# Two-by-two block products with seven multiplications for the outputs of the last three token blocks

## The chip, the cores and the metric

The kernel runs on one core of a Trainium2 chip. The core has five engines with queues of their own: TensorE (PE, matmuls, with its weight loads shown separately as PEld), VectorE (DVE), ScalarE (ACT), GpSimd (POOL) and SyncE (SP, which issues the DMAs). The metric is the time of one execution on the device in microseconds; lower is better. PE reads its operands from the on-chip buffer SBUF and writes sums to PSUM, which has banks of 512 float32 values per partition; POOL works on SBUF only.

## The reference

The program is one transformer layer on 2 x 1024 tokens of width 512: attention, then a gated feed-forward network with weights that are quantised and expanded again, each followed by a normalisation and a residual. Only its last step bears on the change:

```python
    def _L0_ffn_ref(x, w1, w2, w3):
        ...
        gate = jnp.einsum('bsd,hd->bsh', x, dq1)
        up = jnp.einsum('bsd,hd->bsh', x, dq2)
        h = jax.nn.silu(gate) * up
        return jnp.einsum('bsh,dh->bsd', h, dq3)
    x = L0_attn_hidden_states
    x = x + _layernorm(_L0_attn_ref(_layernorm(x, axis=-1), L0_attn_Wq, L0_attn_Wk, L0_attn_Wv, L0_attn_Wo), axis=-1)
    x = x + _layernorm(_L0_ffn_ref(_layernorm(x, axis=-1), L0_ffn_w1, L0_ffn_w2, L0_ffn_w3), axis=-1)
```

The hidden width is 1376, that is ten blocks of 128 and an eleventh of 96. All of it is float32.

## The kernel before

Attention comes first and takes about 1670 us; the feed-forward part after it is the class FeedForward, whose method run drives everything from there on. It goes over four token blocks of 512 tokens (tb = 0 to 3, called block 0 to block 3). Each block has a hidden part and an output part.

In the hidden part, for each of the eleven blocks f of hidden features, the method hidden computes gate and up for 512 tokens. It is already a product of two-by-two blocks by seven multiplications (Strassen's scheme in Winograd's form): seven products, each of two matmuls with 256 columns, on sums of weights (weight_sums, four POOL instructions per f) and sums of tokens (token_sums, four POOL instructions of 512 columns per token block, into the tiles T and into one quarter of the block's transposed tokens xnT). The results, times the sigmoid, become hT[f], 128 hidden features by 512 tokens. The last operation of each f, which multiplies the high half of hT[f] on POOL, is issued one step late, after the next products have begun; for f = 10 it is issued at the end of the hidden part, and token_sums for the next block follows it in POOL's queue.

In the output part, the method outputs takes 128 tokens at a time: eleven matmuls of 512 columns, `lhsT=self.hT[f][:n, m * P : (m + 1) * P]`, `rhs=self.w3[f][:n, :]`, into a bank of the pool "out", then puts three steps into the list later: the statistics of the row (DVE, with a power of -1/2 on POOL, rstd), the normalisation into the row buffer res (DVE), and the addition of the residual yacc with the DMA to the result (DVE, SP). run takes these steps out of later between PE's products; at the end of an output part up to three are left for the first hidden row of the next block, at i = 0, 2 and 4.

PE, DVE, ACT and POOL each work in the order of the program here: every call goes through a wrapper (InOrder) that keeps it. So an instruction waits for its own operands and for everything before it on its engine. The instructions all carry line 117, the wrapper's; operations are told apart by the names of tiles. Names that occur: wos, wkv, wq, ffq, ffqtmp, ffqr, ffqs, ffs are reused buffers that now hold T and hT; wdown, ffqh and ffa hold w3; ffoc is res; pgate, pup, pout and ptr are the PSUM pools "gate", "up", "out" and "tr", of two banks each.

Of the kernel before, what the change touches and what calls it, by code (L numbers as in the profile page):

```python
# [13 lines left out]
F32R = mybir.dt.float32r  # L14
I32 = mybir.dt.int32
AF = mybir.ActivationFunctionType
ALU = mybir.AluOpType
# [4 lines left out]
P = 128  # L22
# [6 lines left out]
KT = HID // P  # L29
CB = 2  # L30
FF = 1376
# [89 lines left out]
def sandwich_kernel(ctx: ExitStack, tc: tile.TileContext, x, wq, wk, wv, wo, w1, w2, w3, out, con):  # L121
    nc = tc.nc
    x = x.rearrange("b n d -> (b n) d")
    out = out.rearrange("b n d -> (b n) d")
# [14 lines left out]
    yacc = keep.tile([P, NCI, HID], F32)  # L139

    xnT = keep.tile([P, KT, T], F32)
# [11 lines left out]
    def norm_stats(src, vector=nc.vector, gpsimd=nc.gpsimd):  # L153

        st = small.tile([P, 6], F32)
        vector.bn_stats(st, src)
        mv = small.tile([P, 2], F32)
        vector.bn_aggr(mv, st)
        ve = small.tile([P, 1], F32)
        vector.tensor_scalar(ve, mv[:, 1:2], EPS, None, ALU.add)  # L160
        rstd = small.tile([P, 1], F32)
        gpsimd.tensor_tensor(rstd, ve, mhalf, ALU.pow)
        return mv[:, 0:1], rstd

    def normed(dst, src, vector=nc.vector, stats=None):
        mean, rstd = stats or norm_stats(src, vector)
        vector.tensor_scalar(dst, src, mean, rstd, ALU.subtract, ALU.mult)
# [131 lines left out]
    def fast_attention():  # L299

        with ExitStack() as attn:
# [6 lines left out]
            q2p = attn.enter_context(tc.tile_pool(name="fq2p", bufs=2))  # L308
# [8 lines left out]
            product = tensor.matmul  # L317
# [5 lines left out]
            def parts_tile(name):  # L323
                return wop.tile([P, 2, GRP, HID], F32R, tag="wop", name=name)
# [85 lines left out]
            keys, Q, S = {}, {}, {}  # L410
# [300 lines left out]
            F = FeedForward((pmm, "mm"), (psc, "sc"), (ptr, "tr"), (po, "o"))  # L711
            early = {}

            def quarters(t):
                return t.rearrange("p i h d -> p (i h) d").bitcast(F32)

            def freed(pool, tag, count, dtype=F32, n=512):

                shape = {F32R: [P, GRP, P], BF16: [P, 576]}.get(dtype, [P, n])
                tiles = [pool.tile(shape, dtype, tag=tag, name=f"ff{tag}{i}", bufs=count) for i in range(count)]  # L720
                if dtype == F32R:
                    return [t.rearrange("p h t -> p (h t)").bitcast(F32) for t in tiles]
                return tiles
# [48 lines left out]
            for n in range(N_):  # L772
                g, b, c = chunks[n]
# [3 lines left out]
                more, keys2 = n + 1 < N_, n + CB < N_  # L777
# [112 lines left out]
            more = [columns(four[:, j, :]) for j in range(4)]  # L890
# [12 lines left out]
            down = quarters(parts_tile("wdown"))  # L903
            for f, t in enumerate([down[:, j, :] for j in range(8)] + freed(q2p, "qh", 2) + freed(q2p, "a", 1)):
                F.w3[f] = t
            F.res = freed(q2p, "oc", 1, F32R)
            F.run(2, 4)

    def general_attention():
# [301 lines left out]
    class FeedForward:  # L1211
# [21 lines left out]
        def next(self, name):  # L1233

            pieces = getattr(self, name)
            i = self.used.get(name, 0)
            self.used[name] = i + 1
            return pieces[i % len(pieces)]
# [152 lines left out]
        def outputs(self, ci):  # L1391
# [10 lines left out]

            self.later += [lambda: stats.append(norm_stats(pf, self.vector, self.gpsimd)), lambda: normed(res, pf, self.vector, stats[0]), added]

        def run(self, f0, ready):


            ups, downs = iter(range(ready, NFT)), iter(range(NFT))

            def loaded_up(f):  # L1410
                return None if f is None else (f, [self.load_up(i, f) for i in range(2)])

            def loaded_down(f):
                return None if f is None else (f, self.load_down(f))

            def next_down(col):
                if col:
                    self.down_weights(*col)
                return loaded_down(next(downs, None))

            row, col = loaded_up(next(ups, None)), loaded_down(next(downs, None))
            last = None
            for tb in range(T // self.TB):
                more = tb + 1 < T // self.TB

                begin = max(f0, 1) if tb == 0 else 1
                xc = self.load_tokens((tb + 1) * self.MB) if more else None
                for f in range(f0 if tb == 0 else 0, NFT):
                    if f not in self.sums:
                        list(self.weight_sums(f))  # L1430
                    products = self.hidden(tb, f)
                    sums = self.weight_sums((f + 1) % NFT) if f + 1 < NFT or more else iter(())
                    m = f - begin if more and f - begin < 2 * self.MB else -1
                    ci = (tb + 1) * self.MB + m // 2
                    if m >= 0 and m % 2 == 0:
                        self.later += self.token_parts(ci, xc)
                    for i in range(7):
                        next(products)
                        if i == 0 and last:
                            next(last)  # L1440
                        if i in (0, 2, 4) and self.later:
                            xn = self.later.pop(0)()
                        if 1 <= i <= 4:
                            next(sums, None)
                        if i == 2 and row:
                            self.up_weights(0, row[0], row[1][0])
                        if i == 4 and row:
                            self.up_weights(1, row[0], row[1][1])
                            row = loaded_up(next(ups, None))
                        if tb == 0 and (i == 5 or i == 1 and f >= NFT - f0):  # L1450
                            col = next_down(col)
                    last = products
                    if m >= 0 and m % 2 == 0:
                        xc = self.load_tokens(ci + 1) if m < 2 * (self.MB - 1) else None
                    elif m >= 0:
                        self.token_transposes(ci, xn)
                next(last)
                last = None
                if more:
                    self.token_sums(tb + 1, self.gpsimd)  # L1460
                for m in range(self.MB):
                    self.outputs(tb * self.MB + m)
                    while len(self.later) > (3 if m + 1 == self.MB and more else 0):
                        self.later.pop(0)()

    def plain_feed_forward():
        with ExitStack() as ffn:
            fp = ffn.enter_context(tc.tile_pool(name="fp", bufs=1))
            psums = [(ffn.enter_context(tc.tile_pool(name=name, bufs=2, space=PSUM)), name) for name in ("pgate", "pup", "ptw", "pout")]
            F = FeedForward(*psums)  # L1470
            quarters = [w[:, j, :] for w in wqs for j in range(4)] + [wos[:, j, :] for j in range(4)]
            quarters += list(tables.rearrange("p i (c e) d -> p (i c) (e d)", e=4)[:, j, :] for j in range(4))
            quarters += [wkv.rearrange("p (j e) d -> p j (e d)", j=2)[:, j, :] for wkv in wkvs for j in range(2)]
            for f in range(NFT):
                for w, name in ((F.w1, "w1"), (F.w2, "w2")):
                    w[f] = [fp.tile([P, KT, P], F32, name=f"{name}_{f}")]
                F.w3[f] = fp.tile([P, 512], F32, name=f"w3_{f}")
                F.hT[f] = quarters.pop() if f < 7 else fp.tile([P, 512], F32, name=f"hT_{f}")
            F.S = [[fp.tile([P, 2, P], F32, name=f"sum{i}{j}") for j in range(4)] for i in range(2)]
            F.tmp = [fp.tile([P, F.HB], F32, name=f"part{j}") for j in range(6)]  # L1480
            F.T = [quarters.pop() for _ in range(3)]
            F.xc, F.yn, F.xn, F.res = ([quarters.pop()] for _ in range(4))
            F.rows, F.cols = ([quarters.pop() for _ in range(2)] for _ in range(2))
            F.sg = [t[:, i * F.HB : (i + 1) * F.HB] for t in (quarters.pop(), quarters.pop()) for i in range(2)]
            for ci in range(F.MB):
                F.tokens(ci, F.load_tokens(ci))
                F.token_transposes(ci, F.token_norms(ci))
            F.token_sums(0, F.gpsimd)
            for f in range(2):
                for i in range(2):  # L1490
                    F.up_weights(i, f, F.load_up(i, f))
            F.scale_products()
            F.run(0, 2)
# [34 lines left out]
    with tc.If(flag != 0) as cmp:  # L1528
        fast_attention()
# [28 lines left out]
```

## Time and profile before

| | us |
|---|---|
| median of the runs (3) | 2101.16 (2100.3 to 2102.02) |
| profiled execution, its own time | 2101.61 |
| its span, first to last instruction | 2099.7 |
| PE busy in the span | 2066.5 (98%) |
| one output part (four outputs) | 37.7 |
| hidden part of blocks 1, 2, 3 | 69.3, 69.4, 66.4 |
| from the last matmul to the end | 8.3 |

The profile is of one execution. A row of the timeline gives start and duration in us, engine, source line, operation, the tile written and the tiles read, shapes (partitions x elements), and in brackets how long the engine had stood idle and what ended that. A row of the table by stretches gives the stretch, its length, and for each engine the busy time with the number of instructions. A float32 matmul appears as two records, each with its own weight load. Matmuls overlap in the pipeline, so what one costs is read from the distance between the starts of neighbours, not from its duration: records of 512 columns start 0.43 us apart and take 0.59 us each.

### The profile page before, as it was taken

What the parts mean: (1) busy time and instruction counts of PE and PEld (TensorE: products, weight loads), DVE (VectorE), ACT (ScalarE), POOL (GpSimd) and SP (SyncE); (2) the same over time, 40 slices, a digit from 0 to 9 for tenths busy, and PEclk for the clock granted to TensorE, in tenths of its full rate; (3) what the DMA queues carried; (4) which work ended last, traced back from release to release, by engine and by line L of the source; (5) the groups of instructions that cost most, each with busy time, mean ns of one, the idle gap of its engine ahead of it and who ended that gap; (6) DMA issues with size and microseconds to landing.
All of it is one profiled execution on the core that took longest, in us unless ns stands there. A gap on an engine that the chain in (4) does not pass through costs nothing.

```text
span 2099.7 us, 29474 instructions
## 1 busy us (share of the span) xinstructions
PE 2066.5 (98%) x9476; PEld 1503.1 (72%) x9476; DVE 1589.6 (76%) x3123; ACT 1394.4 (66%) x4045; POOL 1124.3 (54%) x1524
## 2 busy tenths in 40 slices
PE   7999999999999999999999999999999999999998
PEld 4777777777777777777777777777767785858584
DVE  4888888888888888888888888788887663838352
ACT  4788888887888888888888888888876340202020
POOL 5555655555566546554655574556554452626250
PEclk9999999999999999999999999999999999999999
DMA  6100100010011001000100010000011030000000
GB/s 227 36 11 26 51 16 11 21 51 10 11 40 36 12 15 41 31 11 11 58 13 11 26 58 12 11 17 22 21 36 31 26 101 21 21 20 16 21 1 22
DMA packets 48307, 64.65 MB, mean 31 GB/s; under 512 B 6736, under 2 KB 22736, under 8 KB 48144
## 3 DMA queue, kind: packets, MB, share of 16 engines
q1 hardware_dynamic: 48144, 62.68, 9.3%
q8 instruction: 77, 1.26, 0.2%
q14 instruction: 86, 0.70, 0.1%
HBM read 50.01 MB, written 12.65 MB: 30 GB/s over the span
## 4 chain that ended last, share of the span: by engine, by line
PE 86%; ACT 5%; DVE 5%; POOL 3%; issue 1%; DMA 0%; ACTq 0%; POOLq 0%; DVEq 0%
PE pq L117 18%; PE pout L117 12%; PE py L117 9%; PE pk L117 9%; PE ot L117 9%; PE pa L117 6%; PE ps L117 5%; PE pup L117 3%; PE pgate L117 3%; PE tr L117 3%; PE tq L117 2%; PE pg L117 2%; POOL qr L117 2%; ACT ps L117 1%; PE pS L117 1%
## 5 line engine op out<-in xcount | busy, mean ns | idle before, releaser
L117 POOL TENSOR_TENSOR qtmp<-q,tables 128x512 f32<-128x512 f32 x128 | 162.3, 1268 | 570.6 <-ACT q L117 570.6
L117 PE MATMUL pq<-wq,xnT 128*128 128x512 f32 x1024 | 460.7, 592 | 1.6 <-ACT xnT L117 1.6
L117 PEld LDWEIGHTS pq<-wq,xnT 128*128 128x128 f32 x1024 | 184.8, 190 | 185.4 <-issue 185.4
L117 ACT ACTIVATE zs<-xw,fbounds 128x512 bf16<-128x512 f32 (+3 forms) x416 | 287.8, 723 | 0.0
L117 PE MATMUL py<-wop,oc 128*128 128x512 f32 x1024 | 270.9, 406 | 0.0
L117 ACT ACTIVATE ps<-ps,nms 128x128 f32<-128x128 f32 x512 | 175.1, 342 | 115.4 <-DVE nms L117 101.0
L117 ACT ACTIVATE pq<-pq,nmq 128x128 f32<-128x128 f32 x512 | 175.1, 342 | 91.6 <-DVE nmq L117 79.1
L117 PE MATMUL pk<-wkv,xnT 128*128 128x256 f32 x1024 | 231.5, 379 | 0.0
L117 PEld LDWEIGHTS pk<-wkv,xnT 128*128 128x128 f32 x1024 | 194.5, 190 | 46.5 <-issue 16.3
L117 PEld LDWEIGHTS py<-wop,oc 128*128 128x128 f32 x1024 | 182.9, 189 | 35.0
L117 POOL TENSOR_TENSOR qr<-q,tables 128x256 f32<-128x256 f32 x256 | 206.3, 827 | 0.0
L117 DVE SCALAR_TENSOR_TENSOR zp<-zp,zs 128x512 f32<-128x512 f32 (+3 forms) x224 | 195.2, 871 | 9.9 <-ACT zs L117 4.7
L117 POOL TENSOR_TENSOR qr<-qr,qtmp 128x512 f32<-128x512 f32 x128 | 166.2, 1299 | 10.0
L117 DVE SCALAR_TENSOR_TENSOR zm<-zm,zs 128x512 f32<-128x512 f32 (+3 forms) x192 | 161.5, 841 | 5.0 <-ACT zs L117 2.6
L117 DVE TENSOR_TENSOR ps<-ps,fwin 128x512 f32<-128x512 f32 x128 | 89.2, 697 | 91.2 <-PE ps L117 90.8
L117 PE MATMUL ps<-kT,qrT 128*128 128x128 f32 x1024 | 136.6, 276 | 0.7 <-POOL kT L117 0.5
L117 DVE TENSOR_REDUCE nmq<-pq 128x4 f32<-128x512 f32 x128 | 87.8, 686 | 62.5 <-ACT q L117 61.5
L117 PEld LDWEIGHTS ps<-kT,qrT 128*128 128x128 f32 x1024 | 125.0, 192 | 2.1 <-POOL kT L117 1.2
L117 POOL TENSOR_TENSOR rstd<-ve,mhalf 128x1 f32<-128x1 f32 x62 | 38.5, 622 | 154.3 <-DVE ve L117 154.2
L117 PE MATMUL ot<-qh,S 128*128 128x512 f32 x224 | 114.4, 592 | 0.0
L117 POOL COPY vm<-kv 64x128 f32<-64x128 f32 (+1 forms) x176 | 98.0, 572 | 3.1
L117 ACT ACTIVATION_READ_ACCUMULATOR pq<-pq,nmq 128x1 f32 x512 | 98.8, 193 | 0.0
(311 smaller groups left out, 4584.3 us busy)
## 6 DMA issues: line engine op xcount, KB each, us to landing
wq<-in_L_attn_Wq_dram SPq DMA_DIRECT2D x8, 1024.0 KB, 5.6
wos<-in_L_attn_Wo_dram SPq DMA_DIRECT2D x8, 1024.0 KB, 5.2
wq<-_attn_hidden_states_dram SPq DMA_DIRECT2D x20, 256.0 KB, 2.8
xw<-in_L_ffn_w_dram SPq DMA_DIRECT2D x20, 256.0 KB, 2.6
dq<-zp SPq DMA_DIRECT2D x20, 256.0 KB, 2.0
wos<-dq SPq DMA_DIRECT2D x20, 256.0 KB, 2.6
out_dram<-ffoc SPq DMA_DIRECT2D x16, 256.0 KB, 2.0
tokens<-_attn_hidden_states_dram SPq DMA_DIRECT2D x12, 256.0 KB, 5.1
```

Source lines behind the costliest of these rows:

```text
L117: return lambda *args, **kwargs: self.tc.keep_in_program_order(getattr(self.engine, name)(*args, **kwargs))
```

## The change

The output part of blocks 1, 2 and 3 takes two groups of 128 tokens together (output_pair) and treats them as a product of two-by-two blocks. One side is hT: rows are the two token groups, columns are hidden blocks 0 to 4 and 5 to 9. The other is w3: rows are the same two groups of five hidden blocks, columns are the two halves of 256 output features. Seven products of five matmuls each, of 256 columns, give the four results; the eleventh hidden block is added by one direct matmul per result. The sums of hT that this needs (hidden_sums: S1 and S2 on DVE, S3, which overwrites a21, and S4 on POOL, each five instructions of 128 columns) are computed before the first pair of a block, after token_sums in the program, and for the second pair from inside the first. The sums of w3 (down_sums, down_last: D1, D2, D4 in free buffers and T3 over b12, twenty POOL instructions of 256 columns) are computed once, fifteen during block 0's output part and five during block 1's hidden part. Block 0's outputs are computed as before. The results are added up by DVE and ACT into the row buffers, of which there are now two, the second being the buffer yn; normalisation and residual then work on the row buffer instead of the PSUM bank.

```diff
--- before.py
+++ after.py
@@ -903,7 +903,7 @@
             down = quarters(parts_tile("wdown"))
             for f, t in enumerate([down[:, j, :] for j in range(8)] + freed(q2p, "qh", 2) + freed(q2p, "a", 1)):
                 F.w3[f] = t
-            F.res = freed(q2p, "oc", 1, F32R)
+            F.res = freed(q2p, "oc", 1, F32R) + F.yn
             F.run(2, 4)
 
     def general_attention():
@@ -1402,6 +1402,114 @@
 
             self.later += [lambda: stats.append(norm_stats(pf, self.vector, self.gpsimd)), lambda: normed(res, pf, self.vector, stats[0]), added]
 
+        def down_places(self):
+
+            t = [r[:, i * self.HB : (i + 1) * self.HB] for r in self.rows + self.cols for i in range(2)]
+            t += [xnT[:, kt, i * self.HB : (i + 1) * self.HB] for kt in range(KT) for i in range(2)]
+            self.D1, self.D2, self.D4 = t[0:5], t[5:10], t[10:15]
+
+        def down_block(self, k, j):
+
+            return [self.w3[5 * k + i][:, j * self.HB : (j + 1) * self.HB] for i in range(5)]
+
+        def down_sums(self):
+
+            for i in range(5):
+                (b11, b12), (b21, b22) = ([self.down_block(k, j)[i] for j in range(2)] for k in range(2))
+                for dst, x, y in ((self.D1, b12, b11), (self.D2, b22, self.D1[i]), (self.D4, b21, self.D2[i])):
+                    self.gpsimd.tensor_tensor(dst[i], x, y, ALU.subtract)
+                    yield
+
+        def down_last(self):
+
+            for b12, b22 in zip(self.down_block(0, 1), self.down_block(1, 1)):
+                self.gpsimd.tensor_tensor(b12, b22, b12, ALU.subtract)
+                yield
+
+        def hidden_block(self, c, k):
+            m = c % self.MB
+            return [self.hT[5 * k + i][:, m * P : (m + 1) * P] for i in range(5)]
+
+        def hidden_sums(self, c):
+
+            t = [xnT[:, kt, c // self.MB * self.TB + j * P : c // self.MB * self.TB + (j + 1) * P] for kt in range(KT) for j in range(4)]
+            S1, S2, S4 = t[0:5], t[5:10], t[10:15]
+            (a11, a12), (a21, a22) = ([self.hidden_block(c + i, k) for k in range(2)] for i in range(2))
+            for i in range(5):
+                self.vector.tensor_tensor(S1[i], a21[i], a22[i], ALU.add)
+            for i in range(5):
+                self.vector.tensor_tensor(S2[i], S1[i], a11[i], ALU.subtract)
+                self.gpsimd.tensor_tensor(a21[i], a11[i], a21[i], ALU.subtract)
+            yield S1, S2, S4
+            for i in range(5):
+                self.gpsimd.tensor_tensor(S4[i], a12[i], S2[i], ALU.subtract)
+            yield
+
+        def normed_output(self, ci, res):
+            stats = []
+
+            def added():
+                self.vector.tensor_tensor(res, res, yacc[:, ci, :], ALU.add)
+                nc.sync.dma_start(out[ci * P : (ci + 1) * P, :], res)
+
+            self.later += [lambda: stats.append(norm_stats(res, self.vector, self.gpsimd)), lambda: normed(res, res, self.vector, stats[0]), added]
+
+        def output_pair(self, c, S, ahead):
+
+
+            S1, S2, S4 = S
+            (a11, a12), (S3, a22) = ([self.hidden_block(c + i, k) for k in range(2)] for i in range(2))
+            (b11, T3), (b21, b22) = ([self.down_block(k, j) for j in range(2)] for k in range(2))
+            s1, u2, v, _, _, c22 = self.tmp
+            r0, r1 = self.next("res"), self.next("res")
+            hb, n, m = self.HB, FF - 10 * P, c % self.MB
+            add = lambda dst, x, y: self.vector.tensor_tensor(dst, x, y, ALU.add)
+            taken = lambda: self.later and self.later.pop(0)()
+
+            def product(bank, w, t, more=False, direct=None):
+                for k in range(5):
+                    self.tensor.matmul(bank, lhsT=w[k], rhs=t[k], start=k == 0 and not more, stop=k == 4 and direct is None, skip_group_check=True)
+                if direct is not None:
+                    one(bank, *direct)
+
+            def one(bank, i, j, start=False):
+                lhsT = self.hT[10][:n, (m + i) * P : (m + i + 1) * P]
+                self.tensor.matmul(bank, lhsT=lhsT, rhs=self.w3[10][:n, j * hb : (j + 1) * hb], start=start, stop=True, skip_group_check=True)
+
+            a = self.bank("gate")[:, :hb]
+            product(a, a11, b11)
+            self.scalar.copy(s1, a)
+            taken()
+            cb = self.bank("up")[:, :hb]
+            product(cb, S3, T3)
+            taken()
+            b = self.bank("out")[:, :hb]
+            product(b, S2, self.D2)
+            add(u2, b, s1)
+            taken()
+            d = self.bank("out")[:, :hb]
+            product(d, S1, self.D1)
+            add(v, d, u2)
+            product(a, a12, b21, True, (0, 0))
+            self.scalar.copy(r0[:, 0:hb], a)
+            add(c22, cb, v)
+            taken()
+            S = next(ahead) if ahead else None
+            product(d, S4, b22, True, (0, 1))
+            add(r0[:, hb:], d, u2)
+            self.normed_output(c, r0)
+            taken()
+            if ahead:
+                next(ahead)
+            product(cb, a22, self.D4, True, (1, 0))
+            add(r1[:, 0:hb], cb, u2)
+            taken()
+            e = self.bank("tr")[:, :hb]
+            one(e, 1, 1, True)
+            add(r1[:, hb:], e, c22)
+            self.normed_output(c + 1, r1)
+            return S
+
         def run(self, f0, ready):
 
 
@@ -1419,7 +1527,7 @@
                 return loaded_down(next(downs, None))
 
             row, col = loaded_up(next(ups, None)), loaded_down(next(downs, None))
-            last = None
+            last = down = None
             for tb in range(T // self.TB):
                 more = tb + 1 < T // self.TB
 
@@ -1442,6 +1550,8 @@
                             xn = self.later.pop(0)()
                         if 1 <= i <= 4:
                             next(sums, None)
+                        if i == 5 and down:
+                            next(down, None)
                         if i == 2 and row:
                             self.up_weights(0, row[0], row[1][0])
                         if i == 4 and row:
@@ -1458,9 +1568,24 @@
                 last = None
                 if more:
                     self.token_sums(tb + 1, self.gpsimd)
-                for m in range(self.MB):
-                    self.outputs(tb * self.MB + m)
-                    while len(self.later) > (3 if m + 1 == self.MB and more else 0):
+                if tb == 0:
+                    self.down_places()
+                    down = self.down_sums()
+                    for m in range(self.MB):
+                        self.outputs(m)
+                        for _ in range(4):
+                            next(down, None)
+                        while len(self.later) > (3 if m + 1 == self.MB else 0):
+                            self.later.pop(0)()
+                    down = self.down_last()
+                else:
+                    c = tb * self.MB
+                    sums, ahead = self.hidden_sums(c), self.hidden_sums(c + 2)
+                    S = next(sums)
+                    next(sums)
+                    S = self.output_pair(c, S, ahead)
+                    self.output_pair(c + 2, S, None)
+                    while len(self.later) > (3 if more else 0):
                         self.later.pop(0)()
 
     def plain_feed_forward():
...
```

More of the change, by code (lines that the diff above doesn't have):

```diff
@@ L1482, in plain_feed_forward @@
             F.xc, F.yn, F.xn, F.res = ([quarters.pop()] for _ in range(4))
+            F.res += F.yn
             F.rows, F.cols = ([quarters.pop() for _ in range(2)] for _ in range(2))
```

## The prediction

> **What bounds the kernel now.** I read the busy table of the stages first, because the change touches only the last 365 us. The columns are stretch, length, busy time of TensorE (PE), of its weight loads, of VectorE (DVE), ScalarE (ACT) and GpSimd (POOL), granted clock, DMA share and GB/s. The rows are the outputs of token block 2, the hidden part of block 3, the last outputs, and the tail.
>
> ```profile
> 1949.40:1987.10 37.70, 37.70 (x89) 16.70 (x88) 8.71 (x18) 0.51 (x1) 7.35 (x8) 1.00 0.05 21
> 1987.20:2053.60 66.40, 66.40 (x309) 57.63 (x308) 38.51 (x91) 13.28 (x32) 35.08 (x51) 1.00 0.01 5
> 2053.70:2091.40 37.70, 37.70 (x89) 16.47 (x87) 8.67 (x18) 0.51 (x1) 2.36 (x4) 1.00 0.06 22
> 2091.40:2099.70 8.30, 0.19 (x1) 0.00 (x0) 2.54 (x5) 0.00 (x0) 0.55 (x1) 0.82 0.10 38
> ```
>
> PE is busy for the whole of each output part and the others hardly at all. So work taken off PE counts in full, and so does every wait put in its way. Next the timeline at the seam where the outputs of block 2 begin (PE starts them at 1949.42): POOL's own queue there.
>
> ```profile
> 1951.21 0.72 POOL L117 TENSOR_TENSOR ffs<-ffex,wq 96x256 f32<-96x256 f32 x1 [2.46 <-DVE wq L117]
> 1951.90 1.26 POOL L117 TENSOR_TENSOR wos<-xnT 128x512 f32<-128x512 f32 x1
> 1953.24 1.26 POOL L117 TENSOR_TENSOR xnT<-xnT 128x512 f32<-128x512 f32 x1
> 1954.46 1.27 POOL L117 TENSOR_TENSOR wos<-xnT,wos 128x512 f32<-128x512 f32 x1
> 1955.81 1.27 POOL L117 TENSOR_TENSOR wkv<-xnT,wos 128x512 f32<-128x512 f32 x1
> ```
>
> The first is the last hidden row, which waits for PE, DVE, ACT and DVE in turn; then come the four sums of the next block's tokens (token_sums). POOL is free only 7.66 us after PE began the outputs. Today PE waits for none of this. Two more views price a contention and the clock: DVE and POOL side by side, and the granted clock (seventh figure) around an early gap of PE and after its last matmul.
>
> ```profile
> 1890.80 0.88 DVE L117 TENSOR_TENSOR yacc<-wq 128x512 f32<-128x512 f32 x1
> ```
> ```profile
> 1891.09 1.18 POOL L117 TENSOR_TENSOR ffzs<-wup 128x256 f32<-128x256 f32 x1
> 1892.24 0.72 POOL L117 TENSOR_TENSOR ffzs<-wup,ffzs 128x256 f32<-128x256 f32 x1
> ```
> ```profile
> 28.00:29.00 1.00, 0.28 (x1) 0.29 (x2) 0.30 (x2) 0.66 (x4) 0.92 (x2) 0.66 1.06 404
> 34.00:35.00 1.00, 1.00 (x7) 1.00 (x6) 0.00 (x0) 0.11 (x1) 0.99 (x1) 0.50 1.03 362
> 35.00:36.00 1.00, 1.00 (x8) 0.87 (x7) 0.13 (x1) 0.00 (x0) 0.92 (x3) 0.93 1.06 387
> 2096.50:2097.00 0.50, 0.00 (x0) 0.00 (x0) 0.00 (x0) 0.00 (x0) 0.00 (x0) 0.79 0.16 53
> ```
>
> **The change, part by part.** The sum is made on the profiled execution, 2101.61 us (span 2099.7); the median shown is 2101.16, 0.45 lower.
>
> **Matmuls, -12.3.** Each output takes 9.44 us (four in 37.76, from 1949.42 to 1987.18), a pair 18.88. A pair now takes 7 products of 5 matmuls plus 4 single ones, 39 of 256 columns. The hidden part shows such matmuls without a gap: 77 products of 2 in 66.47 us, 0.4316 each. So 39 x 0.4316 = 16.83, 2.05 less, and six pairs give 12.3. Weight loads double in number, but the hidden part carries the same load per matmul (57.63 us of 66.40) without stalling.
>
> **The second product of blocks 1 and 2, +14.4.** In output_pair PE does A11*B11 (five matmuls, 2.16 us) and then S3*T3. S3 = a11-a21 is computed on POOL, and hidden_sums is called after token_sums, so it lies behind the five POOL instructions shown. Rows of 512, 256 and 192 columns at 1.26, 0.72 and 0.59 us lie on a line that gives 0.455 us for 128 columns, one every 0.42 back to back (192 columns start 0.55 apart, 256 columns 0.68). Undisturbed, the first S3 is there at 7.66 + 0.455 = 8.1 and the fifth at 9.8. But ten DVE sums of two SBUF inputs run meanwhile, and the pair of rows above shows that they and POOL's take turns: 1.18 against 0.72, 0.46 for 512 columns, so 0.115 for 128. Six turns before the first S3 put it at 8.8, and the next follow every 0.535, the fifth at 10.95. With 0.1 to wake PE, the product ends at 11.5 instead of 4.3: 7.2 per block, 14.4 for two. Bounds: no turns at all, 6.0 per block; DVE's whole 0.285 us (its rows of 512 and 256 take 0.69 and 0.42) for all ten, 8.9. I take the row's own stretch. Everything behind S3*T3 on PE waits too; S2 (DVE), S1 and S4 are done before their products come up in that late order.
>
> The Trainium skill, "SBUF — State Buffer", section "SBUF: two separate sides", says that a DVE operation with two SBUF inputs and a GpSimd operation exclude each other for the whole instruction. By that rule it is the upper bound, 8.9 per block and 3.4 more in the sum; the row shows only 0.46 of DVE's 0.88 lost, so the row is taken.
>
> **The clock after that wait, +4.0.** PE stands still from 2.2 to 8.9, some 6.7 us. In the rows above the clock fell to half after 2.3 us of idling at the start (last matmul before it until 26.0, fall near 28.3) and after 5 at the end (2091.6 to 2096.6), so 6.7 should be enough. It stayed low until 35.07, 6.4 us after PE resumed at 28.71 with gaps, and 3.6 after its last gap ended at 31.47. At half clock a matmul is 0.863. If low for 3.6 us, the product and its successors end 1.4 later than above (4.2 of five matmuls done, the rest at 0.43); if for 6.4, 2.7. Middle 2.0, twice 4.0. Bounds per block: 0, if the clock does not fall, and 2.7.
>
> The skill's "TensorE: Matmul & The Clock Gate" (Part 1) puts both directions at a free-running window of about 3.4 us; by it the low stretch is an estimated 3.4 to 6.8 us and the sum 2.6 to 6.0 instead of 4.0.
>
> **Block 3's first pair, +1.5.** No token_sums there. The last hidden row on POOL ends 2.54 after PE begins (2055.47 + 0.72 against 2053.65); the first S3 follows at 3.15, the fifth at 5.3, and the product ends at 5.8 instead of 4.3. Bounds 0.9 and 2.4, as above. The idling is one microsecond, so the clock holds. The second pair of every block has its sums made one pair ahead (asked for after C22, some 8 us before they are needed) and waits for nothing: ten DVE sums of 0.285 and ten POOL sums of 0.455 lie beside 16.8 us of PE. Without that cover the 1.5 would come three times more.
>
> **The tail, +1.65.** At the end DVE now does, after the last product, R1's low half (0.42), the norm of R0 (0.65 to 0.81), R1's high half (0.42) and R0's residual (0.69) before the last row's statistics start: 2.0 us after PE's end, where they now start 0.2 after it. The rest of the tail (8.3 us) stays, the DMA of R0 being issued 3 us ahead of the last one. Bounds 1.2 and 2.5.
>
> **Sums of w3 and small things, +0.3.** Fifteen POOL sums of 256 columns (0.68 apart, 10 us) go into block 0's outputs, four after each, where POOL has 30 us free of 37.7; an rstd behind them is late by up to 2.7 us, but PE has a second pout bank and 9.4 us. Uncovered they would cost 10. Five more (0.72 each) go into block 1's hidden rows, where POOL works 45.0 of 69.3 us and sits idle before each row's last operation. That row already loses about 1 us to DVE, so I take 0.3 of their 3.6; bounds 0 and 3.5. DVE enters the next hidden part about 1.7 us later; its C22 is then ready at 4.8 where PE wants it at 5.2. Residual rows now share yn's buffer: its output DMA is issued near 5.6 and lands by 7.8 (2.0 us), and yn is written near 8.5. SP issues as many output DMAs as before.
>
> Sum: -12.3 + 14.4 + 4.0 + 1.5 + 1.65 + 0.3 = +9.55 on 2101.61, or about **2110.7** on the median. All lower bounds together give +1.8, all upper ones +19.3.
>
> **Rivals.**
>
> A: the clock does not fall, or the sums take no turns. For: the end of the trace needed 5 us to fall, and the wait is only a little longer. Against: the start needed 2.3. Time without the 4.0: 2106.7; without turns too (6.0 a block, 0.9 at the last) 2103.7.
>
> B, the other side: POOL does not stand in the way, because S3 reaches PE before A11*B11 ends. Then only the gain, the last block's 1.5 per block and the tail count: -12.3 + 4.5 + 1.65 + 0.3 = -5.85, 2095.3. It decides where the whole loss per block (wait and clock) is under (12.3 - 1.5 - 1.65 - 0.3)/2 = 4.4 us; token_sums alone is 5.2 on POOL. For it: only a program order other than the one in the code. Against: the rows show the order, and every engine of this part is driven in program order.
>
> C: worse. The product waits for all five S3 before its first matmul, and the clock is low for the full 6.4 us: 1.7 and 0.7 more per block, or block 1's hidden rows pay the 3.5: 2114 to 2119.
>
> D: the change's matmuls do not reach 0.4316. Nothing speaks for it but the doubled weight loads; 0.01 each would cost 234 x 0.01 = 2.3.
>
> **How the numbers follow.** My case 0.60 (own range 2107 to 2114), A 0.15, B 0.08, C and D 0.17. A difference of 0.2% (4.2 us) is about what a measurement of this kernel tells from none. Faster is B, 0.08; within 0.2% (up to 2105.4) is the lower half of A and a sliver of the rest, 0.10; slower 0.82. Range 2103 to 2117: it takes in most of A and half of C.
>
> **What would show it.** Right: in blocks 1 and 2 PE's longest wait, some 6.5 us, is put down to a POOL subtraction of hT pieces, with the granted clock at 0.5 for 4 us or more after it; output parts of about 43, 43 and 35 us where 37.76 stood; pairs without a wait near 16.8. Wrong: a wait under 4 us there, a clock that holds, or PE waiting elsewhere (for S4, for a bank, for yn). What would mislead me most is the time of a 128-column sum on POOL and DVE, which no row of this trace shows.

## The result and the profile after

The changed kernel takes 2107.99 us (median of 7 runs, 2106.51 to 2109.32) against 2100.82 for the kernel before in the same comparison (2100.30 to 2102.02): a ratio of 1.0034, 95% interval 1.0024 to 1.0043. It is slower by a third of a percent. The forecast was 2110.7 in a range of 2103 to 2117. The profiled execution took 2107.65 us, its span is 2105.8.

The first view is the table by stretches; its columns are explained at the start of the prediction (the clock is the third figure from the right). The rows are the outputs of block 1, hidden part 2, outputs 2, hidden part 3, outputs 3 and the tail.

```profile
1840.90:1883.00 42.10, 35.95 (x158) 30.94 (x158) 21.73 (x47) 2.00 (x5) 17.13 (x28) 0.92 0.04 13
1883.00:1952.80 69.80, 69.52 (x326) 58.66 (x324) 57.28 (x131) 15.19 (x36) 45.48 (x63) 1.00 0.06 20
1952.80:1995.20 42.40, 36.25 (x157) 31.19 (x156) 21.64 (x47) 2.00 (x5) 17.12 (x28) 0.92 0.04 13
1995.20:2061.70 66.50, 66.50 (x309) 57.77 (x309) 39.99 (x95) 13.28 (x32) 35.62 (x51) 1.00 0.02 9
2061.70:2096.70 35.00, 34.27 (x157) 29.03 (x155) 18.76 (x47) 2.00 (x5) 12.05 (x24) 1.00 0.04 16
2096.70:2105.80 9.10, 0.15 (x1) 0.00 (x0) 3.75 (x9) 0.00 (x0) 0.55 (x1) 0.63 0.17 65
```

Read from the starts of PE's records, three output parts of 37.78 us each are now 42.05, 42.43 and 34.98. In the first two PE is idle for some 6.15 us, and their clock is 0.92. Only the third comes near what the smaller number of matmuls would bring, 33.70 (two pairs of 16.85). The other parts of the block loop have hardly moved (hidden parts 69.51, 69.81 and 66.48, before 69.45, 69.45 and 66.48).

PE's waits of the whole feed-forward part (what waited, for whom, us in total, times, the longest) name the place. The three instances are one per block, 6.2, 6.2 and 0.7 us:

```profile
PE pup L117 <- POOL wq L117: 13.0, 3, 6.2
PE pup L117 <- DVE ffzx L117: 0.4, 2, 0.2
```

The timeline of PE at the seam of block 1 (output part from 1840.94). pgate is A11*B11, pup is S3*T3, the first pout is S2*D2:

```profile
1842.67 0.59 PE L117 MATMUL pgate<-wdown,wkv 128*128 128x256 f32 x2
1849.42 3.78 PE L117 MATMUL pup<-wdown,wq 128*128 128x256 f32 x8 [6.16 <-POOL wq L117]
1852.99 0.79 PE L117 MATMUL pup<-wdown,wkv 128*128 128x256 f32 x2
1853.62 0.59 PE L117 MATMUL pout<-wkv,xnT 128*128 128x256 f32 x2
```

S3*T3 begins 8.48 us after the start of the part and takes 4.20 us instead of 2.16. POOL's queue meanwhile: the last hidden row, four token sums, and only then S3 (four of its five pieces in one line).

```profile
1842.76 0.72 POOL L117 TENSOR_TENSOR ffs<-ffex,ffqrT 96x256 f32<-96x256 f32 x1 [2.45 <-DVE ffqrT L117]
1843.44 1.25 POOL L117 TENSOR_TENSOR wos<-xnT 128x512 f32<-128x512 f32 x1
1844.78 1.39 POOL L117 TENSOR_TENSOR xnT<-xnT 128x512 f32<-128x512 f32 x1
1846.13 1.30 POOL L117 TENSOR_TENSOR wos<-xnT,wos 128x512 f32<-128x512 f32 x1
1847.51 1.39 POOL L117 TENSOR_TENSOR wkv<-xnT,wos 128x512 f32<-128x512 f32 x1
1848.87 1.88 POOL L117 TENSOR_TENSOR wq<-wq 128x128 f32<-128x128 f32 x4
```

The first piece is ready at 1849.36 (it took 0.50 us), and PE starts 0.06 later. The clock in the stretches around it, again by the table, with the low stretch of block 2 as the last row:

```profile
1843.00:1846.50 3.50, 0.26 (x2) 0.00 (x0) 3.50 (x4) 0.37 (x1) 3.42 (x4) 1.00 0.00 0
1846.50:1853.20 6.70, 3.78 (x9) 3.06 (x10) 3.93 (x6) 0.00 (x0) 6.62 (x12) 0.50 0.01 2
1853.50:1883.00 29.50, 29.50 (x139) 25.92 (x138) 12.83 (x34) 1.12 (x3) 6.83 (x13) 1.00 0.05 18
1959.20:1966.00 6.80, 4.73 (x11) 3.83 (x12) 3.09 (x6) 0.00 (x0) 5.80 (x12) 0.50 0.00 0
```

In block 1 it falls to half after 3.3 us of idling (1843.26 to 1846.55) and comes back 3.9 us after PE has resumed, just before S3*T3 ends; in block 2 PE resumes at 1961.27, and the clock comes back 4.7 us later. After 1853.5 PE does not wait once: the second pair of the block runs from 1866.14 to 1882.99, 16.85 us.

### The profile page after: what moved, and what is told of

Same layout as the page of the kernel before. It is cut to its first block, busy times and chain, and to the rows that moved or that the text cites. A ratio compares the mean times of both kernels' runs of the same rounds, so it can differ in the third digit from the quotient of the medians.

```text
span 2105.8 us, 30135 instructions
## 1 busy us (share of the span) xinstructions
PE 2058.5 (98%) x9680; PEld 1543.8 (73%) x9680; DVE 1630.4 (77%) x3219; ACT 1398.7 (66%) x4057; POOL 1170.6 (56%) x1604
## 4 chain that ended last, share of the span: by engine, by line
PE 85%; ACT 5%; DVE 5%; POOL 4%; issue 1%; DMA 0%; ACTq 0%; POOLq 0%; DVEq 0%
PE pq L117 18%; PE pk L117 9%; PE py L117 9%; PE pout L117 9%; PE ot L117 8%; PE pa L117 6%; PE ps L117 5%; PE pup L117 5%; PE pgate L117 4%; PE tr L117 3%; PE tq L117 2%; PE pg L117 2%; POOL qr L117 2%; ACT ps L117 1%; PE ptr L117 1%
## 5 line engine op out<-in xcount | busy, mean ns | idle before, releaser
L117 ACT ACTIVATION_READ_ACCUMULATOR ps<-ps,nms 128x1 f32 x512 | 98.7, 193 | 0.0
```

What stands on the lines that cost most here:

```text
L117: return lambda *args, **kwargs: self.tc.keep_in_program_order(getattr(self.engine, name)(*args, **kwargs))
```

## Experiments

All times are medians, each beside runs of the kernel before on the same chip (2101.17 in the first four, 2101.03 in the last two). The ratios and their intervals are worked out from the single executions and can differ by three ten-thousandths from the quotient of the two medians.

**The sums of hT ahead of the token sums.** This separates POOL's queue order from everything else that happens at the seam.

```diff
-                if more:
+                if more and tb == 0:
                     self.token_sums(tb + 1, self.gpsimd)
...
                     S = next(sums)
                     next(sums)
+                    if more:
+                        self.token_sums(tb + 1, self.gpsimd)
                     S = self.output_pair(c, S, ahead)
```

> The only edit to the changed kernel: in blocks 1 and 2 the sums of hT for the first pair come ahead of the next block's four token sums in POOL's queue. If PE's wait is POOL's queue order, blocks 1 and 2 become like block 3 of the changed kernel (34.98 us of output part where 42.05 and 42.43 stood, a wait of about 0.7 us, granted clock 1.00 throughout): 2107.99 - 14.5 - 0.3 = 2093.2 us, some 7.6 below the kernel before. If the wait is instead the late end of the last hidden row or the sums themselves, the wait stays near 6 us and the time near 2108.

Measured: 2093.48 us, 0.9966 of the kernel before (0.9953 to 0.9978). All three output parts are 34.98 us with a full clock, and POOL's and PE's rows of block 1 show the order (output part from 1841.21):

```profile
1843.03 0.72 POOL L117 TENSOR_TENSOR ffs<-ffex,ffqrT 96x256 f32<-96x256 f32 x1 [2.45 <-DVE ffqrT L117]
1843.72 0.91 POOL L117 TENSOR_TENSOR wq<-wq 128x128 f32<-128x128 f32 x2
```
```profile
1844.27 2.25 PE L117 MATMUL pup<-wdown,wq 128*128 128x256 f32 x8 [0.73 <-POOL wq L117]
```
```profile
1841.20:1876.20 35.00, 34.27 (x158) 29.22 (x157) 19.73 (x47) 2.00 (x5) 16.96 (x28) 1.00 0.04 16
```

The last hidden row is as late as ever, 1.8 us after the part began, and the sums are the same; only the four token sums ahead of them now come after them. So the order of two calls was worth 14.5 us (7.07 and 7.45 in the two output parts), and with it turned the change is a gain of 7.7.

**The wait filled with matmuls.** This takes the fallen clock away and leaves the wait.

```diff
+            if ahead and c < NCI - self.MB:
+                fill = self.bank("tr")[:, :hb]
+                for i in range(14):
+                    self.tensor.matmul(fill, lhsT=a11[i % 5], rhs=b11[i % 5], start=i == 0, stop=i == 13, skip_group_check=True)
             cb = self.bank("up")[:, :hb]
             product(cb, S3, T3)
```

> The order of the changed kernel, but PE is given 14 matmuls of 256 columns (6.0 us) into an unused bank between the first and the second product of blocks 1 and 2; their result is used by nothing. If the fallen clock is a cost of its own, the second product now runs at the pace of POOL's sums and ends about 10.75 us after the start of the output part instead of 12.7 and 13.1: 2107.99 - 4.2 = 2103.8. If the clock costs nothing there because POOL paces the product anyway, the time stays at 2108.

Measured: 2103.67 us, 1.0013 (1.0003 to 1.0023). The rows are both output parts, with a clock of 1.00:

```profile
1840.00:1880.20 40.20, 40.06 (x185) 34.51 (x184) 21.67 (x47) 2.00 (x5) 17.17 (x28) 1.00 0.04 14
1950.00:1990.30 40.30, 40.15 (x186) 34.57 (x186) 22.09 (x47) 2.00 (x5) 17.07 (x28) 1.00 0.04 13
```

PE does six microseconds of useless work in each and is 4.3 us faster. By the starts of the records the parts are 40.23 us each, so the fallen clock costs 1.82 and 2.20, and the wait alone 40.23 - 2 x 16.85 = 6.53 per block. S3*T3 begins 8.51 us after the start of the part, where it began at 8.48, so the matmuls put in do not delay it.

**Pairs in block 3 alone.** One part of the change by itself: the outputs of blocks 1 and 2 as before, the last five sums of w3 in hidden part 3.

```diff
-                    down = self.down_last()
+                elif more:
+                    for m in range(self.MB):
+                        self.outputs(tb * self.MB + m)
...
+                    if tb == 2:
+                        down = self.down_last()
                 else:
```

> Only block 3 is computed with pairs; blocks 1 and 2 as in the kernel before. The fifteen sums of w3 stay in block 0, the other five move to block 3's hidden part. By the trace of the changed kernel block 3 gains 2.78 us and the tail loses 0.82: 2.0 below the kernel before, 2098.8. If the gain of a pair depended on blocks 1 and 2, or the sums of w3 cost more than they show, it would be nearer 2101 or above.

Measured: 2098.67 us, 0.9991 (0.9982 to 1.0000). The rows are hidden part 3 and its outputs:

```profile
1985.40:2051.80 66.40, 66.40 (x309) 57.63 (x308) 39.61 (x91) 13.26 (x32) 39.00 (x56) 1.00 0.01 5
2051.80:2086.80 35.00, 34.27 (x157) 29.04 (x156) 18.75 (x47) 2.00 (x5) 12.06 (x24) 1.00 0.05 17
```

The five sums of w3 appear in POOL's column (39.00 us and 56 instructions; 35.08 and 51 before) and add nothing to PE's 66.40. The output part is the 34.98 us that it is in the changed kernel, so the gain of a pair does not hang on the other blocks. This is read from the trace; the interval of the whole time reaches 1, and by itself it would not show a gain.

**Sums first, and the products reordered.** A version meant to be the fastest: what needs no sum of hT goes first.

```diff
             product(a, a11, b11)
             self.scalar.copy(s1, a)
             taken()
+            e = self.bank("tr")[:, :hb]
+            one(e, 1, 1, True)
+            product(a, a12, b21, True, (0, 0))
+            self.scalar.copy(r0[:, 0:hb], a)
+            taken()
             cb = self.bank("up")[:, :hb]
             product(cb, S3, T3)
+            self.scalar.copy(c22, cb)
             taken()
+            d = self.bank("out")[:, :hb]
+            product(d, S1, self.D1)
+            add(v, d, c22)
             b = self.bank("out")[:, :hb]
             product(b, S2, self.D2)
             add(u2, b, s1)
...
+            add(v, v, u2)
+            add(r1[:, hb:], e, v)
...
```

> As the run with the sums first, and in each pair the products that need no sum of hT (a11 b11, the single matmul of the fourth result, a12 b21) come first, then S3 T3, S1 D1, S2 D2, S4 b22, a22 D4; C22 is put together from copies so that no accumulation waits for it, and the last product feeds only half a row. The second product's operands are ready when PE comes to it, so an output part is 33.7 us plus about 0.25 for each of two waits for the copy of the first product, 34.2: three times -3.55 against the kernel before, tail +0.2: 2100.8 - 10.4 = 2090.4. If the weight loads or the banks bind, it stays above 2093.

Measured: 2091.82 us, 0.9958 (0.9944 to 0.9972); 1.4 above the expectation. The output parts are 34.39 us, where 34.2 was expected, and the tail is 9.1 us instead of 8.5. DVE's rows at the end (PE is done at 2079.62) show why:

```profile
2079.45 0.55 DVE L117 TENSOR_SCALAR ffoc<-ffoc,mv,rstd 128x512 f32<-128x512 f32 x1 [0.66 <-POOL rstd L117]
2080.03 0.69 DVE L117 TENSOR_TENSOR ffoc<-ffoc,yacc 128x512 f32<-128x512 f32 x1
2080.64 0.42 DVE L117 TENSOR_TENSOR wq<-pup,ffzx 128x256 f32<-128x256 f32 x1
2081.09 0.69 DVE L117 BATCH_NORM_STATS2 st<-wq 128x6 f32<-128x512 f32 x1
```

The norm and the residual of the row before stand ahead of the last addition, so the last row's statistics start 1.5 us after PE's end, no earlier than in the changed kernel.

**Two small edits on top.** The lines are shown against the run above.

```diff
-            taken()
-            taken()
+            if c + 2 < NCI:
+                taken()
+                taken()
             product(cb, a22, self.D4, True, (1, 0))
             add(r1[:, 0:hb], cb, u2)
             self.normed_output(c + 1, r1)
+            if c + 2 == NCI:
+                self.later.insert(0, self.later.pop(2))
...
+            for step in (ready, mixed) if ahead else (mixed, ready):
+                step()
```

Here ready is the block of A12*B21 and the single matmul, mixed that of S3*T3.

> The reordered version with two small edits: the second pair of a block, whose S3 is long ready, does S3 T3 right after a11 b11, so that the copy of a11 b11 is done before a12 b21 accumulates on it (0.36 us less in each of three blocks); and in the very last pair the statistics of the last row are taken before the norm and the residual of the row before it (0.4 us less in the tail). If these waits are what separates the reordered run (2091.82) from its 39 matmuls per pair, this one takes 2090.3; if the second pair then waits for something else, it stays at 2091.8.

Measured: 2090.34 us, 0.9952 (0.9938 to 0.9965). Output parts 34.05, 34.04 and 34.04, tail 8.74, where the run above had 34.39 and 9.1. It has the lowest median here, 10.7 us under the kernel before, though only 1.5 under the run above, whose own executions spread by as much; by the times alone the two are not told apart, and the difference rests on the traces. What remains above 33.70 lies in the first two records of A12*B21 in each first pair, which start 0.25 and 0.10 us late; the weight load before them is released by ACT's copy of A11*B11.

**Two more sums in POOL's queue.** The opposite of the first run: more in front of S3.

```diff
+                    if more:
+                        for i in range(2):
+                            self.gpsimd.tensor_tensor(self.xn[0], yacc[:, c, :], yacc[:, c + 1, :], ALU.add)
                     S = next(sums)
                     next(sums)
                     S = self.output_pair(c, S, ahead)
```

> The changed kernel with two more POOL sums of 512 columns (some 1.3 us each, into an unused buffer, their result used by nothing) between the token sums and the sums of hT in blocks 1 and 2. If POOL's queue sets the wait, the second product starts 2.6 us later in each of the two blocks, 11.1 us after the output part begins instead of 8.5: 2107.99 + 5.2 = 2113.2, with 1.5 either way for where the clock returns. If something else that is merely as late as POOL sets it, the time changes by less than 2 us.

Measured: 2114.69 us, 1.0063 (1.0050 to 1.0077). S3*T3 begins 11.22 us after the part's start in both blocks, 2.74 later than in the changed kernel. The waits of the feed-forward part and the clock of block 1:

```profile
PE pup L117 <- POOL wq L117: 18.5, 3, 8.9
```
```profile
1847.10:1857.20 10.10, 3.64 (x9) 2.93 (x10) 6.09 (x7) 0.00 (x0) 9.94 (x15) 0.50 0.01 2
```

PE follows POOL's queue in full: 2.74 us is what the two sums take up in it. The output parts are 44.67 and 45.45 us; together 5.6 longer, of which 5.5 are the later start. The clock is low for longer, but mostly while PE idles, which costs nothing: it comes back 3.7 and 5.3 us after PE resumes, against 3.9 and 4.7 in the changed kernel. The medians differ by 6.7, 1.1 more than the two parts; the profiled execution is 1.35 later already where block 0's outputs begin, in code that the edit does not touch.

## Why the prediction was right, and where its sizes were off

The forecast held in sign, place and mechanism. Its terms against what the traces and runs show, in us:

| step of the prediction | forecast | measured | from |
|---|---|---|---|
| matmuls | -12.3 | -12.2 | second pairs take 16.85; 3 x (33.70 - 37.78) |
| second product of blocks 1 and 2 | +14.4 | +13.1 | filled wait: 6.53 per block |
| the clock after that wait | +4.0 | +4.0 | 1.82 and 2.20, changed kernel less filled wait |
| block 3's first pair | +1.5 | +1.3 | 34.98 - 33.70 |
| the tail | +1.65 | +0.9 | from PE's last matmul on, 9.16 against 8.24 |
| sums of w3 and small things | +0.3 | +0.4 | hidden part 1 +0.06, part 2 +0.36, part 3 unchanged |

The measured terms add up to +7.5. The spans differ by 6.2, but the profiled execution of the changed kernel reached block 0's outputs 1.28 us earlier (1733.65 against 1734.93), in code that the change does not touch; from there to the end the difference is 7.5, and the medians differ by 7.2.

Two terms came out by luck. The clock's 4.0 was the middle between two readings of one stretch, 1.4 and 2.7 per block, and the two blocks lie 0.2 on either side of it. The last row has the right size in the wrong place: the forecast put its 0.3 on the five sums of w3 in hidden part 1, and that part grew by 0.06. The 0.36 lie in hidden part 2, which holds none of these sums, and they come with pairs in block 1: this part takes 69.63 to 69.85 in all runs with them, and 69.45 in the run with pairs in block 3 alone. They are lost in its first 17 us, where the forecast held that a later DVE costs nothing and where PE now waits 0.2 us for a DVE sum; what makes up the rest was not tested.

Some readings of the prediction were off by little. An output part was 37.78 us, not 37.76. A clock of 0.93 over the microsecond from 35 on means 0.14 us at half clock, so the clock came back at 35.14, not 35.07, and by the same working it fell at 2096.8 at the end, not 2096.6. And the 128-column sum that no row was said to show stands in the attention part of that trace: 128 of them on POOL (tile kr), 0.451 us at the least and 0.465 in the middle, which is the 0.455 that the prediction took from its line.

The largest error is in the second product, 1.3 us for both blocks, and its step is the turns of DVE and POOL. The prediction charged POOL 0.115 us for each of six turns, and a pitch of 0.535 from one S3 piece to the next after that. DVE's rows in the changed kernel show who pays:

```profile
1842.60 0.28 DVE L117 TENSOR_TENSOR xnT<-wq,wkv 128x128 f32<-128x128 f32 x1
1842.80 2.04 DVE L117 TENSOR_TENSOR xnT<-wq,ffq 128x128 f32<-128x128 f32 x1
1844.77 0.28 DVE L117 TENSOR_TENSOR xnT<-wq,ffqtmp 128x128 f32<-128x128 f32 x1
1844.97 1.34 DVE L117 TENSOR_TENSOR xnT<-wq,ffqr 128x128 f32<-128x128 f32 x1
```

A DVE sum that takes 0.28 us alone takes 2.04 when it meets two POOL instructions, the last hidden row and a token sum. POOL's token sums take 1.25 to 1.39 against 1.26 undisturbed. So POOL's first S3 came 8.4 us after the start of the part instead of 8.8, and S3's pieces came 0.46 apart; over four of them that is 0.3, and the two make up the 0.7 per block. Stretching a 512-column row down to 128 columns overstated POOL's loss. The Trainium skill's rule of the whole instruction ("SBUF — State Buffer", "SBUF: two separate sides"), which the prediction set aside in favour of the row, describes DVE's side of these rows well: DVE waits out whole POOL instructions. It does not describe POOL's side, which loses at most 0.14 of DVE's 0.28; as an estimate for the wait, the 8.9 us per block that it gave were 2.4 too many.

The tail was over by 0.7. The term that was too large is "R1's low half, the norm of R0, R1's high half and R0's residual", 2.0 us: R1's low half starts 0.2 us before PE's end, these DVE instructions overlap at their ends, and the norm reads the row from SBUF in 0.54 us where it took 0.81 from PSUM. The statistics of the last row start 1.5 us after PE's end, and its own norm is shorter too, so the rest of the tail did not stay as it was. The norms are R0's and the last row's in the changed kernel, and the last row's in the kernel before:

```profile
2096.80 0.54 DVE L117 TENSOR_SCALAR ffoc<-ffoc,mv,rstd 128x512 f32<-128x512 f32 x1
2098.19 0.69 DVE L117 BATCH_NORM_STATS2 st<-wq 128x6 f32<-128x512 f32 x1
2099.94 0.55 DVE L117 TENSOR_SCALAR wq<-wq,mv,rstd 128x512 f32<-128x512 f32 x1 [0.66 <-POOL rstd L117]
```
```profile
2093.40 0.81 DVE L117 TENSOR_SCALAR ffoc<-pout,mv,rstd 128x512 f32<-128x512 f32 x1 [0.66 <-POOL rstd L117]
```

Of the rivals, A fails on the clock: it fell in both blocks, and the turns took place, though they cost less. B, that POOL does not stand in the way, fails on the wait of 6.2 us; its point of decision, a loss per block under 4.4 us, is confirmed from the other side by the run with the sums first, where the loss is 1.3 and the kernel is faster. C fails because PE started on the first piece of S3, 0.06 us after it was written, the clock was low for 3.9 and 4.7 us of work and not for 6.4, and hidden part 1 paid 0.06 and not 3.5. D fails on the second pairs, 39 matmuls in 16.85 us. "What would show it" asked for 4 us or more of low clock after the wait; it was 3.9, just under, and 4.7.

## What to carry to other kernels

When an engine that was idle is given work that the bottleneck waits for, its queue at that moment decides, not its busy share: POOL was free for 30 of 37.7 us, and the change lost 14.5 us because its sums stood behind four instructions that nobody needed for another 30 us. So order each queue by when its results are wanted, and let the bottleneck begin with what needs no preparation. And a wait of TensorE can cost more than its length: each wait of 6.2 us cost 2 us more through the clock, while in the waits of 0.7 us the clock held.

## What the runs showed of the hardware that had not been expected

The low stretches of the clock at the waits are 6.8 us in the changed kernel (1846.55 to 1853.37 and 1959.19 to 1966.01) and 10.2 us with the two more sums (1847.04 to 1857.28 and 1963.09 to 1973.33), two and three times 3.41; the early one in the kernel before, of which the prediction shows rows, is 6.8 too. The two falls in the changed kernel lie 112.64 us apart, 33 times 3.413. The Trainium skill, "TensorE: Matmul & The Clock Gate", Part 1, describes a free-running window of 3413 ns, and these lengths and this distance agree with it. So in these runs the longer wait lengthened the low stretch by a whole step, and how long the clock stayed low after the wait went by where in a step PE resumed and not by the length of the wait: 3.9 and 4.7 us after waits of 6.2 us, 3.7 and 5.3 after waits of 8.9.

Six microseconds of useless matmuls in a wait made the kernel 4.3 us faster. The expectation of that run had worked it out from the changed kernel's trace (2103.8); nothing in the prediction had pointed to it.
